# A gated state-space and mixture-of-experts layer: the tile pipeline, the decays and the norm in another order

## The chip, the cores and the metric

The kernel runs on one core of a Trainium2 chip. The metric is the device time of one execution in microseconds (us). The engines of the core work side by side, each through its own queue in order: PE (TensorE, matrix products and transposes), DVE (VectorE), ACT (ScalarE), POOL (GpSimd) and SP (SyncE, which here only issues DMAs). They wait for each other by semaphores. Products land in PSUM, in banks of 128 x 512 float32.

## The reference, cut to what matters

There are four batches of 512 rows and 512 columns. A selective state-space layer runs over a context and is gated with the normed rows; then a mixture of experts runs over the result.

```python
# state-space layer: 512 channels, 16 states each, 512 time steps
u = silu(causal_conv4(in_proj_w @ ctx))
dt_lo, Bm, Cm = split(x_proj_w @ u)
delta = softplus(dt_proj_w @ dt_lo + dt_proj_b)
state = state * exp(delta_t * A) + (delta_t * u_t) * B_t      # for each t
y_t   = sum over the states of state * C_t
y     = (y + D * u) * silu(layernorm(x))
x     = x + tanh(g_xattn) * y
# mixture of experts: one shared, 3 of 7 routed, weighted by their renormed probabilities
h     = layernorm(x)
f(h, w1, wg, w2) = (silu(h @ w1) * (h @ wg)) @ w2
x     = x + tanh(g_ffn) * (f(h, shared) + sum over 3 experts of weight * f(h, expert))
```

All of it is float32.

## The kernel before

**Recurrence** (`loop`, L433). Channels lie on partitions in four chunks `c` of 128, time along the free axis. The 16 states are taken two at a time (`NG`), so one batch has 8 x 4 = 32 *steps*. Step n has these pieces. POOL forms the products `h` = B * (delta u) (`product`, L499). ACT forms two decays exp(delta * A) into PSUM (`decay`, L508; two buffers, `ps_a`). DVE scans twice along time (L533). Then comes `finish` (L456), which runs at the head of the next step: DVE multiplies `h` by C (L465) and adds the two states to `y` (L476). In batch 0, PE adds the states up instead. At the end of the batch each chunk is gated (`gate`, L454). For batches 1 to 3 each decay is issued right before its scan (L532). `finish` also carries pieces of the preparation of the batch after next (`ahead`, L332: projections, convolution, softplus), and issues the next load of B and C rows (`load_bc`).

**Norm** (`post`, L583). For the batch just gated, four row blocks `t` are transposed by PE (L592), added to x by DVE with their statistics (L594 to L596), scaled (`row_scale`, a power on POOL), normed (L604), transposed back (L609) and copied by ACT (L610).

**Experts** (`experts`, L853). `route` (L620) computes the router: product `pl`, transposes `pg`, about forty small DVE operations with an exponential on ACT and the product `pc` in between, ending in `table` (which expert each tile of 128 rows belongs to). POOL then scatters the normed rows into tiles in HBM (L738, 12 DMAs). Meanwhile PE computes the shared expert: four pairs of products `p1s` and `p2s` (`half`), silu by ACT (`sgs`), the multiply by DVE (`hidden`, L880), and the second product `pos` (`second`). Then come 13 tiles, each with three 1 MB weights loaded for its expert. A tile i is cut into three slots of the loop at L954: first `p1`; then the silu, the transpose of the gated rows of tile i-1, and `p2`; then the copy of that transpose (`turned_h`), the multiply h * p2 (L1000), the transpose and copy of the next tile's input (`pt_x`, `turned_x`), and the output product `po` of tile i-1. Two slots later ACT scales it (`out_scaled`, L816), and POOL adds it into HBM by an accumulating scatter (`add_rows`, L821). More tiles than 13 run in a branch (`rest`, L832).

**Order.** The order on each queue is written out by the program: while batch b is in `post` and `experts`, the steps of batch b+1 are put between the slots. The loop at L1063 does this with two running sums. Each slot yields its planned time on PE (tP) and on DVE (tV); steps are issued while tV is behind tP, or once where a slot says so. The tile slots are planned at `SLOT` = 3.5 (L851) and 4.1 us. `moe` (L1029) runs all of `post` for a batch, after its recurrence has ended, and then `experts`.

Of the kernel before, what the change touches and what calls it, by code (L numbers as in the profile page):

```python
# [32 lines left out]
def gated_ssm_moe(  # L33
# [170 lines left out]
    class Layer:  # L204
# [6 lines left out]
        def __init__(self, b, u, delta, y):  # L211
            self.b, self.u, self.delta, self.y = b, u, delta, y
            self.pin, self.pdt, self.z, self.ln = {}, {}, {}, {}
            self.n_rest = self.n_soft = self.n_du = self.n_mul = 0
            self.bcs, self.hs = {}, {}
# [217 lines left out]
    def loop(b, sums):  # L433
# [5 lines left out]
        u, delta, y = ly.u, ly.delta, ly.y  # L439
# [6 lines left out]
        elif nxt is not None:  # L446
            todo = ahead(nxt)
        szs = None
# [7 lines left out]
        def finish(n, h):  # L456
# [9 lines left out]
            if sums is None:  # L466
                if b - 1 in shared_done:
                    cost += next(todo, 0.0)
# [39 lines left out]
        def decay(n, j):  # L508
            g0, c = steps[n]
            da = ps_a.tile([P, L], F32, tag="da", name=f"da_{b}_{g0}_{c}_{j}")  # L510
            nc.scalar.activation(da, delta[:, c, :], AF.Exp, scale=a_neg[:, c, g0 + j : g0 + j + 1])  # L511
            return da
# [3 lines left out]
        for n, (g0, c) in enumerate(steps):  # L516
# [6 lines left out]
            das = []  # L523
            if b == 0:
                das = [decay(n, j) for j in range(NG)]
# [5 lines left out]
            for j in range(NG):  # L531
                da = das[j] if das else decay(n, j)  # L532
                nc.vector.tensor_tensor_scan(h[:, j, :], da, h[:, j, :], 0.0, ALU.mult, ALU.add)  # L533

            if n < last:
                product(ly, n + 1)
            elif nxt is not None and nxt.n_mul > 0:
                product(nxt, 0)
            if b == 0 and g0 == 0:
# [28 lines left out]
        if b == 0:  # L568
            cost += ready(nxt, 0)
            product(nxt, 0)  # L570
        loop_done.add(b)
# [11 lines left out]
    def post(q):  # L583

        b, t0, nt = CHUNKS[q]
# [3 lines left out]
        for t in range(nt):  # L589
            pt = spare(f"pt_{q}_{t}")  # L590
            for c in range(NC):
                nc.tensor.transpose(pt[:, ts(c, P)], y[:, c, ts(t0 + t, P)], ident)  # L592
            x_t = xx[:, t0 + t, :]
            nc.vector.scalar_tensor_tensor(x_t, pt, tg[:, 0:1], x_t, ALU.mult, ALU.add)  # L594
            nc.vector.bn_stats(st[:, t, :], x_t)
            nc.vector.bn_aggr(mv[:, t, :], st[:, t, :])  # L596
            yield 1.7, 1.7
        rstd = row_scale(mv, f"f_{q}")
        xnT = layers[b].u[:, :, 0 : nt * P]
        xns = one.tile([P, NC, D + NW], F32, tag="xn", name=f"xn_{q}")  # L600
        yield 1.5, 1.5, True
        for t in range(nt):
            xn = xns[:, t, 0:D]
            nc.vector.tensor_scalar(  # L604
                xn, xx[:, t0 + t, :], mv[:, t, 0:1], rstd[:, t : t + 1], ALU.subtract, ALU.mult
            )
            pn = spare(f"pn_{q}_{t}").rearrange("p (c q) -> p c q", c=NC)
            for c in range(NC):
                nc.tensor.transpose(pn[:, c, :], xn[:, ts(c, P)], ident)  # L609
            nc.scalar.copy(xnT[:, :, ts(t, P)], pn)  # L610
            yield 1.0, 1.0
# [3 lines left out]
        )  # L615
        normed[q] = xnT, xns
# [3 lines left out]
    def route(q):  # L620
# [28 lines left out]
        nc.scalar.activation(pb, pb, AF.Exp)  # L649
        s2 = tile_("s2", [nt])  # L650
# [118 lines left out]
    def turn(src, what):  # L769
        pt = ps_t.tile([P, NC, P], F32, tag="pt", name=f"pt_{what}")  # L770
# [61 lines left out]
    def rest(q, i, table, n, into):  # L832

        with tc.If(n > i):
# [4 lines left out]
            xT = turned(turn(rows_in(q, i), f"x_{what}"), f"x_{what}")  # L839
# [5 lines left out]
            hT = turned(turn(h, f"h_{what}"), f"h_{what}")  # L845
# [5 lines left out]
    SLOT = 3.5  # L851

    def experts(q):  # L853
# [10 lines left out]
        W = {-1: ws}  # L864
# [4 lines left out]
        def sgs(hc, p1):  # L869
            sg = two.tile([P, L], F32, tag="sg", name=f"sgs_{q}_{hc}")  # L870
            nc.scalar.activation(sg[:, 0:M], p1[:, 0:M], AF.Silu)
            return sg

        def half(k, hc):
            pool, tag = (((ps_h, "p1"), (ps_o, "po")), ((ps_h, "p2"), (ps_t, "pt")))[k][hc % 2]
            return mm(
                pool, tag, f"p{k + 1}s_{q}_{hc}", lambda c: ws.t[k][:, c, ts(hc, P)], lambda c: xnT[:, c, :], M
            )

        def hidden(hc):  # L880
            p2, sg = p2s.pop(hc), sg_s.pop(hc)
            nc.vector.tensor_tensor(hTs[:, hc, :], sg[:, 0:M], p2[:, 0:M], ALU.mult)  # L882


        p2s, sg_s = {}, {}
# [3 lines left out]
        for hc in range(NC):  # L889
            if hc == 0:  # L890
                next(way)
            elif hc > 1:
                next(way, None)
# [228 lines left out]
```

## Time and profile before

| quantity | value |
|---|---|
| three runs | 1179.94, 1183.39 and 1183.77 us; median 1183.39 |
| profiled execution, its own time | 1183.39 us |
| its span, first to last instruction | 1181.3 us |
| PE busy | 962.1 us (81%) |
| DVE busy | 815.8 us (69%) |
| ACT busy | 536.4 us (45%) |
| POOL busy | 471.1 us (40%) |
| mean granted PE clock | 0.929 |
| DMA | 276.29 MB, mean 234 GB/s |

The profile's second part cuts the span into 40 equal slices of 29.5 us; each digit is the busy share in tenths, and PEclk is the PE clock that was granted. Rows of groups give a line, an engine, an operation, what it writes and reads, how often, and the mean time of one. A row of waits names who waited, for whom, and for how long in total, how often and at most. In a row of the timeline the square bracket says how long the engine had been idle before it, and what ended that. PE's ends are modelled, since its products are pipelined.

### The profile page before, as it was taken

Reading aid. Unit: us, or ns where it says so; the run is one execution under the profiler, and the core shown is the slowest. Engines: PE = TensorE matmul, PEld = TensorE weight load, DVE = VectorE, ACT = ScalarE, POOL = GpSimd, SP = SyncE. Lnnn points to the kernel's source line nnn. Section 1 sums busy time; section 2 is a strip of 40 time slices with the busy share of each in tenths; the row PEclk is TensorE's granted clock in tenths of the full one; section 3 lists DMA queues with packets and bytes.
Section 4 is the critical chain, followed back from the end, with each engine's and each line's share of the span. In section 5 each row is a group of like instructions: output and inputs, shape, how many; then the busy total and the mean of one; then the engine's idle time right before and its main releaser. Section 6 shows DMA issues by size and latency. Waiting matters only on the chain. (4 is left out here: it accounts for less than half of the span.)

```text
span 1181.3 us, 8876 instructions
## 1 busy us (share of the span) xinstructions
PE 962.1 (81%) x2504; PEld 431.3 (37%) x2504; DVE 815.8 (69%) x1093; ACT 536.4 (45%) x746; POOL 471.1 (40%) x311
## 2 busy tenths in 40 slices
PE   7475654889998973989998875888998959999995
PEld 3121222334443432434443333333444434444442
DVE  5888995788977787779977787979898723100000
ACT  5654332337667661436676662336566511112211
POOL 0256641463453534464554442645556314011111
PEclk9689896989999996999998896999999989999998
DMA  4169210487988981399997781587998935889994
GB/s 128 41 225 376 78 67 18 173 259 241 337 305 266 316 272 45 142 306 305 339 301 263 274 274 44 195 291 260 314 363 300 312 88 205 287 288 320 314 322 102
DMA packets 138426, 276.29 MB, mean 234 GB/s; under 512 B 17262, under 2 KB 17262, under 8 KB 138110
## 3 DMA queue, kind: packets, MB, share of 16 engines
q1 hardware_dynamic: 126846, 248.91, 60.7%
q0 software_dynamic: 11328, 26.42, 9.3%
q8 instruction: 26, 0.43, 0.1%
q10 hardware_dynamic: 192, 0.26, 0.1%
q14 instruction: 34, 0.28, 0.1%
HBM read 234.85 MB, written 44.91 MB: 237 GB/s over the span
## 5 line engine op out<-in xcount | busy, mean ns | idle before, releaser
L503 POOL TENSOR_TENSOR h<-bc,home 128x1024 f32<-128x1024 f32 x128 | 301.9, 2364 | 356.9 <-DVE home L476 266.4
L783 PE MATMUL p<-w,turned_x 128*128 128x512 f32 x832 | 376.8, 596 | 13.1 <-DMA w<-in_w_dram 7.0
L533 DVE TENSOR_TENSOR_SCAN h<-da,h 128x512 f32<-128x512 f32 x256 | 298.5, 1207 | 73.4 <-ACT da L511 67.5
L783 PE MATMUL po<-w,turned_h 128*128 128x512 f32 x416 | 199.7, 625 | 30.0 <-ACT turned_h L777 30.0
L511 ACT ACTIVATE da<-home,a_neg 128x512 f32<-128x512 f32 x256 | 171.2, 687 | 114.8 <-DVE h L533 113.0
L783 PEld LDWEIGHTS p<-w,turned_x 128*128 128x128 f32 x832 | 153.3, 191 | 191.1 <-issue 173.5
L821 POOL DMA_INDIRECT acc<-yo,row x52 | 94.4, 1816 | 189.9 <-ACT yo L816 153.3
L1000 DVE TENSOR_TENSOR h<-h,p 128x512 f32<-128x512 f32 x52 | 35.1, 674 | 155.0 <-PE p L783 151.2
L476 DVE TENSOR_TENSOR home<-home,h 128x512 f32<-128x512 f32 x192 | 134.8, 702 | 5.8
L465 DVE TENSOR_TENSOR h<-h,bc 128x1024 f32<-128x1024 f32 x96 | 125.8, 1310 | 1.2
L783 PEld LDWEIGHTS po<-w,turned_h 128*128 128x128 f32 x416 | 79.3, 200 | 117.0 <-issue 82.9
L474 PE MATMUL sum<-hc,ident 128*128 128x512 f32 x128 | 72.0, 693 | 54.1 <-DVE hc L465 54.1
L816 ACT ACTIVATE yo<-po,weight 128x512 f32<-128x512 f32 x52 | 35.7, 686 | 130.4 <-PE po L783 130.4
L738 POOL DMA_INDIRECT xs<-xn,place x48 | 58.6, 1220 | 89.7 <-issue 73.2
L777 ACT COPY turned_x<-pt_x 128x512 f32<-128x512 f32 x52 | 30.5, 586 | 119.8 <-PE pt_x L772 119.5
L924 PE MATMUL pos<-w_s,home 128*128 128x512 f32 x128 | 59.4, 620 | 7.8 <-DVE home L882 6.1
L511 ACT ACT_TABLE_LOAD x49 | 62.9, 1283 | 1.7 <-ACT xd L252 0.7
L474 PEld LDWEIGHTS sum<-hc,ident 128*128 128x128 f32 x128 | 24.1, 208 | 101.0 <-DVE hc L465 81.6
L783 PE MATMUL p1s<-home,w_s 128*128 128x512 f32 x128 | 60.0, 613 | 0.0
L783 PE MATMUL p2s<-home,w_s 128*128 128x512 f32 x128 | 57.9, 594 | 1.2 <-DVE home L882 1.1
L984 ACT ACTIVATE h<-p 128x512 f32<-128x512 f32 x52 | 31.1, 597 | 60.7 <-PE p L783 60.5
L984 ACT ACT_TABLE_LOAD x39 | 50.0, 1283 | 16.0 <-PE p L783 15.4
(136 smaller groups left out, 796.8 us busy)
## 6 DMA issues: line engine op xcount, KB each, us to landing
w<-in_w_dram SPq DMA_DIRECT2D x104, 1024.0 KB, 7.5
w<-in_wg_dram SPq DMA_DIRECT2D x52, 1024.0 KB, 11.7
bc<-rows SPq DMA_DIRECT2D x32, 1024.0 KB, 8.4
xt<-xs SPq DMA_DIRECT2D x52, 256.0 KB, 6.3
xs<-empty SPq DMA_DIRECT2D x6, 1560.0 KB, 16.0
w_s<-in_ws_dram SPq DMA_DIRECT2D x8, 1024.0 KB, 10.5
xx<-in_x_dram SPq DMA_DIRECT2D x4, 1024.0 KB, 9.6
w_s<-in_wsg_dram SPq DMA_DIRECT2D x4, 1024.0 KB, 12.8
```

The costliest lines, as they stand in the source:

```text
L465: nc.vector.tensor_tensor(hc, h, bc[:, 1], ALU.mult)
L474: nc.tensor.matmul(sums[c], ident, hc[:, j, :], start=False, stop=(g0 + j == NS - 1))
L476: nc.vector.tensor_tensor(y[:, c, :], y[:, c, :], h[:, j, :], ALU.add)
L503: nc.gpsimd.tensor_tensor(h, layer.bcs[g0][:, 0], layer.u[:, c, :].unsqueeze(1).to_broadcast([P, NG, L]), ALU.mult)
L511: nc.scalar.activation(da, delta[:, c, :], AF.Exp, scale=a_neg[:, c, g0 + j : g0 + j + 1])
L533: nc.vector.tensor_tensor_scan(h[:, j, :], da, h[:, j, :], 0.0, ALU.mult, ALU.add)
L738: put = nc.gpsimd.indirect_dma_start(xs[q % 2], bass.IndirectOffsetOnAxis(ap=place[:, t, k : k + 1], axis=0), xns[:, t, :], None)
L783: nc.tensor.matmul(p[:, 0:n], lhs(c), rhs(c), start=(c == 0), stop=(c == NC - 1))
L816: nc.scalar.activation(yo, po, AF.Copy, scale=slot_of[q][0][:, i : i + 1])
L821: nc.gpsimd.indirect_dma_start(acc, bass.IndirectOffsetOnAxis(ap=slot_of[q][1][:, i : i + 1], axis=0), yo, None, compute_op=ALU.add,)
L924: nc.tensor.matmul(pos[t], hTs[:, c, ts(t, P)], ws.t[2][:, c, :], start=(c == 0), stop=(c == NC - 1))
L984: nc.scalar.activation(h, p1, AF.Silu)
```

## The change

Five things change in the order of the work. The arithmetic stays.

1. A decay pair belongs to a layer and a step (`decay(layer, n)`), and is issued after the scans of the step before, also across two batches.
2. A tile is still three slots, with the stages placed as follows: `gated(i-1)`, `copy_h(i-2)` and `p1(i)`; then `out(i-3)`, the next input's transpose and `p2(i)`; then its copy, the silu, `turn_h(i-1)`, `output(i-2)` and `add_rows` for tile i-3. Two slots follow the last tile. Weight loads move with their buffers' last readers. The shared expert is regrouped in the same way, and the router's sum gets a slot after its exponential. In the branch `rest`, two transposes use other PSUM banks.
3. `post` works on pairs of row blocks in six pieces, with more planned steps between.
4. `moe` issues pieces of the next batch's `post` after each slot of `experts`, as soon as that batch's recurrence has ended.
5. `SLOT` goes from 3.5 to 3.75; the pieces of `ahead` are issued one or more per step, by how many are left.

```diff
         def finish(n, h):
...
                 if b - 1 in shared_done:
-                    cost += next(todo, 0.0)
+                    left = max(n_todo - done[0], 0)
+                    for _ in range(max(1, -(-left // max(1, len(steps) - NC - n)))):
+                        done[0] += 1
+                        cost += next(todo, 0.0)
...
-        def decay(n, j):
+        def decay(layer, n):
             g0, c = steps[n]
-            da = ps_a.tile([P, L], F32, tag="da", name=f"da_{b}_{g0}_{c}_{j}")
-            nc.scalar.activation(da, delta[:, c, :], AF.Exp, scale=a_neg[:, c, g0 + j : g0 + j + 1])
-            return da
+            layer.das[n] = []
+            for k in range(g0, g0 + NG):
+                da = ps_a.tile([P, L], F32, tag="da", name=f"da_{layer.b}_{k}_{c}")
+                nc.scalar.activation(da, layer.delta[:, c, :], AF.Exp, scale=a_neg[:, c, k : k + 1])
+                layer.das[n].append(da)
...
-            for j in range(NG):
-                da = das[j] if das else decay(n, j)
+            for j, da in enumerate(ly.das.pop(n)):
                 nc.vector.tensor_tensor_scan(h[:, j, :], da, h[:, j, :], 0.0, ALU.mult, ALU.add)
             if n < last:
                 product(ly, n + 1)
+                decay(ly, n + 1)
             elif nxt is not None and nxt.n_mul > 0:
                 product(nxt, 0)
+                decay(nxt, 0)
...
     def post(q):
...
+        each(turn_y, pairs[0])
+        yield 1.6, 0.0
+        for k, pair in enumerate(pairs):
+            each(add_y, pair)
+            if k + 1 < len(pairs):
+                each(turn_y, pairs[k + 1])
+                yield 1.6, 3.2
         rstd = row_scale(mv, f"f_{q}")
...
+        yield 0.0, 3.4, True
+        each(norm, pairs[0])
+        yield 0.0, 1.4
+        for k, pair in enumerate(pairs):
+            if k > 0:
+                each(copy_xn, pairs[k - 1])
+            else:
+                for more in pairs[1:]:
+                    each(norm, more)
+            each(turn_xn, pair)
+            yield 1.8, (1.4 if k == 0 else 0.0)
+        each(copy_xn, pairs[-1])
...
     def route(q):
...
         nc.scalar.activation(pb, pb, AF.Exp)
+        yield
         s2 = tile_("s2", [nt])
...
-    SLOT = 3.5
+    SLOT = 3.75
...
         for hc in range(NC):
...
+            if hc > 0:
+                sgs(hc - 1)
+            next(way, None)
+            half(0, hc)
+            yield part, (2.8 if hc == 1 else 0.0), hc == 1
+            if hc > 0:
+                hidden(hc - 1)
+            next(way, None)
             if hc == 1:
...
+            half(1, hc)
+            yield part, (0.4, 4.8, 0.7, 0.7)[hc], hc < 3
...
+        def gated(i):
+            nc.vector.tensor_tensor(hs[i], hs[i], p2.pop(i), ALU.mult)
+        def turn_h(i):
+            pth[i] = turn(hs.pop(i), f"h_{q}_{i}")
+        def copy_h(i):
+            hT[i] = turned(pth.pop(i), f"h_{q}_{i}")
+        def output(i):
+            po[i] = mm(ps_o, "po", f"po_{q}_{i}", lambda c: hT[i][:, c, :], lambda c: W[i].t[2][:, c, :])
+        def out(i):
+            yos[i] = out_scaled(q, i, po.pop(i))
+        for i in range(last_tile + 1):
+            if i > 0:
+                gated(i - 1)
+            if i > 1:
+                copy_h(i - 2)
+            p1[i] = mm(ps_h, "p1", f"p1_{what}", lambda c: xT[i][:, c, :], lambda c: W[i].t[0][:, c, :])
...
+            if i > 0 and i + 1 <= last_tile:
                 W[i + 1].load(1)
+            if i > 2:
+                W[i - 1].load(2)
...
+            yield SLOT, 0.7
+            if i > 2:
+                out(i - 3)
+            if i < last_tile:
+                ptx[i + 1] = turn(xt.pop(i + 1), f"x_{q}_{i + 1}")
+            p2[i] = mm(ps_h, "p2", f"p2_{what}", lambda c: xT[i][:, c, :], lambda c: W[i].t[1][:, c, :])
...
+            yield SLOT + 0.6, 0.0
+            if i < last_tile:
+                xT[i + 1] = turned(ptx.pop(i + 1), f"x_{q}_{i + 1}")
+            hs[i] = two.tile([P, D], F32, tag="sg", name=f"h_{what}")
+            nc.scalar.activation(hs[i], p1.pop(i), AF.Silu)
+            flush()
+            if i > 0:
+                turn_h(i - 1)
+            if i + 2 <= last_tile:
+                W[i + 2] = tile_weights(q, i + 2, table)
+                W[i + 2].load(0)
+            if i > 1:
+                output(i - 2)
+            if i > 2:
+                add_rows(q, i - 3, yos.pop(i - 3))
             if i == last_tile:
+                W[i].load(2)
...
+            yield SLOT + 0.6, 0.0
         i = last_tile
+        gated(i)
+        out(i - 2)
+        copy_h(i - 1)
+        output(i - 1)
+        turn_h(i)
+        yield SLOT + 0.6, 0.7
+        add_rows(q, i - 2, yos.pop(i - 2))
+        copy_h(i)
+        out(i - 1)
+        output(i)
+        yield SLOT, 0.0
+        add_rows(q, i - 1, yos.pop(i - 1))
+        out(i)
+        add_rows(q, i, yos.pop(i))
...
     def moe():
+        posts = [post(q) for q in range(len(CHUNKS))]
...
-            yield from post(q)
+            yield from posts[q]
             banks = SOME
-            yield from experts(q)
+            for slot in experts(q):
+                yield slot
+                if q + 1 < len(CHUNKS) and CHUNKS[q + 1][0] in loop_done:
+                    others, banks = banks, SOME[:2]
+                    piece = next(posts[q + 1], None)
+                    banks = others
+                    if piece is not None:
+                        yield piece
```

## The prediction

> **What bounds the kernel now.** I read the busy shares in slices first, then the busy time by stage, then the waits inside one stage, then single rows. The slices show where engines idle:
>
> ```profile
> PE   7475654889998973989998875888998959999995
> DVE  5888995788977787779977787979898723100000
> PEclk9689896989999996999998896999999989999998
> ```
>
> Until slice 6 only the recurrence of batch 0 runs. From slice 33 on only the tiles of batch 3 run, and PE is full. Between them lie batches 0 to 2, where neither engine is: each dip of PE (slices 7, 16 and 25) is the norm ahead of a batch. I cut the span there, with columns of span, then busy of PE, weight load, DVE, ACT and POOL, PE clock, DMA share and GB/s:
>
> ```profile
> 261.00:454.00 193.00, 166.68 (x447) 75.47 (x447) 161.69 (x196) 122.21 (x168) 86.25 (x40) 0.95 0.84 276
> 454.00:466.00 12.00, 3.53 (x16) 3.16 (x17) 11.12 (x19) 0.00 (x0) 3.45 (x3) 0.64 0.16 56
> 466.00:523.00 57.00, 50.07 (x131) 22.27 (x129) 47.24 (x81) 21.35 (x29) 31.00 (x30) 0.98 0.54 189
> 523.00:713.50 190.50, 167.54 (x448) 76.03 (x448) 159.19 (x191) 121.05 (x166) 85.39 (x39) 0.94 0.88 290
> 783.00:951.00 168.00, 152.27 (x412) 70.27 (x411) 136.83 (x159) 96.54 (x129) 81.11 (x37) 0.97 0.92 307
> 951.00:962.60 11.60, 1.99 (x17) 1.73 (x16) 6.88 (x15) 0.69 (x1) 2.70 (x3) 0.88 0.31 53
> 1016.80:1163.00 146.20, 143.25 (x404) 67.06 (x404) 9.99 (x18) 28.54 (x49) 17.16 (x11) 1.00 0.91 291
> ```
>
> Three stages repeat in each batch: a front (454 to 466 for batch 1: add, norm), the shared expert with the routing (466 to 523), and 13 tiles (523 to 713). The last row is the same 13 tiles with nothing beside them: 11.2 us a tile, PE busy 98%. In batches 0 to 2 the tiles take 193, 190 and 168 us, while DVE idles 31 us in each. In the two engines' waits in 523 to 713 (total, times, longest) the same name stands on both sides:
>
> ```profile
> DVE h L533 <- ACT da L511: 22.7, 9, 6.0
> PE po L783 <- ACT turned_h L777: 11.2, 4, 5.2
> ```
>
> ACT is only 64% busy there. It works in order: a decay queues behind tile work, and a copy for PE behind decays. One instance:
>
> ```profile
> 660.76 1.42 DVE L476 TENSOR_TENSOR home<-home,h 128x512 f32<-128x512 f32 x2
> 663.91 1.15 ACT L291 ACTIVATE ln<-z 128x512 f32<-128x512 f32 x2
> 666.36 1.30 ACT L511 ACTIVATE da<-home,a_neg 128x512 f32<-128x512 f32 x2
> 667.15 2.34 DVE L533 TENSOR_TENSOR_SCAN h<-da,h 128x512 f32<-128x512 f32 x2 [4.97 <-ACT da L511]
> 667.60 0.57 ACT L777 COPY turned_h<-pt_h 128x512 f32<-128x512 f32 x1
> 668.23 6.09 PE L783 MATMUL po<-w,turned_h 128*128 128x512 f32 x8 [5.24 <-ACT turned_h L777]
> ```
>
> DVE is through at 662.2 and stands until 667.15; PE stands 5.24 us for a copy of 0.57 us behind the same decays, then runs its eight matmuls in 6.09 us where unbroken tiles take 3.44. So the tiles of batches 0 to 2 are bound by this coupling, not by an engine.
>
> **The change part by part.** "Step" is one pass of the recurrence on DVE: multiply 1.22, two adds 1.42, two scans 2.34, together 4.98 us.
>
> *Decays a step ahead.* No instruction is added. The decay of step n+1 now follows scan n in ACT's queue. A decay buffer is still freed only by a scan (two buffers), so the lead is what DVE does in between, 2.64 us; it covers two decays (1.30) and one table load (1.28). What is queued behind the waiting decay is ACT's tile work (silu, copies, `out`), and PE waits for that. I expect it bearable, because each of these now has a slot (some 3.9 us of PE) before its consumer. Bounds per tile phase: nothing gained, or all 31 us of DVE's idle.
>
> *A slot between producer and consumer.* Work per tile is the same: 24 matmuls at 0.43 us (eight in 3.44) and two transposes of 0.44, 11.2 us. `gated` of tile i goes from its third slot to the first of tile i+1, `output` one tile later. The third weight of a tile is asked for after its buffer's last reader; before, SP stood 124 us in 434 to 713 on just that (its wait for `po`), with the other loads behind it. Exception: the last tile's third weight is issued one slot (about 5 us) before use, and 1 MB took 7.5 us to land. In batches 0 and 1 that hides under DVE's rest; in 2 and 3 I charge 2 and 1 us (at most 5).
>
> *What a tile phase is then worth.* Each is counted to the gate that ends the next recurrence (batch 2: to its last matmul). Batch 0: DVE 161.7 less one step that moved into the front, 157. Batch 1: PE 145.6, plus 13.7 for the next batch's projections (32 matmuls at 0.43), less two outputs that now lie behind the gate (7) = 152; DVE 159.2 less two steps = 149. Batch 2: 145.6 of tiles and 5.5 of transposes moved in (1.94 at 953.6 and 3.67 at 962.7 in batch 3's norm now) = 151. On each I put half of the idle before, since two engines near the same load don't mesh perfectly: 15.5, 15.5, and 8 for PE in batch 2 (168 less 152.3), and there the 2 us above. That gives **172, 168, 161** for 193, 190, 168.
>
> *The rule against it.* The Trainium skill, "ScalarE: Activation LUTs", section "What ACT_TABLE_LOAD costs", charges 2.66 us for every switch of tables, drain included. The changed order still switches about twice a tile. In 523 to 713 there are 29 loads; at 1.38 us more each, ACT's 121 us would be 161, nothing could be hoped for from reordering, and I would leave 190 (some 20 us more on the sum). But the row says 1283 ns, and at 591.67 a load of 1.28 us is followed by a decay at 592.97: no drain. I take the row.
>
> *DMA.* The tiles of batches 0 to 2 move 53, 55 and 52 MB (GB/s times span). At 172, 168 and 161 us that is 310 to 328 GB/s. By the shares of 0.84, 0.88 and 0.92 the engines would be full at 162, 168 and 155 us: hardly any room. "Perfetto Trace Analysis", section "Identifying the Most-Contended Engine", holds that occupancy of the 16 engines misleads and bytes count. The trace leans that way: a stretch from 835 to 885 moved 345 GB/s at 0.98, one from 1060 to 1110 only 322 at 0.99 with PE hardly waiting. At 345 the floors are 154, 160 and 150, below my sum. I take those; by occupancy I would add 10.
>
> *The fronts* grow, since `post` now issues a second step (batch 2: a third) before the norm. Batch 1, from the gate: scans 2.34, four adds with statistics 6.4 (0.72, 0.69, 0.18 each), a step with one product 5.7, small ones: 15. But `rstd` on POOL now stands behind the last two accumulating scatters, each waiting for the one before to land (8.4 us median): about 19, for 11.2 before. Batch 2: `rstd` stands ahead of these, but there are three steps: 21 for 11.1. Batch 0: the longer steps of the start give 24 for 19.3. The steps themselves are not lost; they were taken off above.
>
> *Shared expert.* The router's exponential, waited for 3 to 5.4 us before, gets a step to hide it. But a step now also stands before the table: in batch 1 the table is ready 28.6 us after the first `pn` instead of 22.5. The 12 scatters on POOL (4.7 us per three, with two products of 2.35 between) end at 52 instead of 48.5, then 5.3 to the load and 2.7 to the transpose as at 514 to 522: first tile after 61.5 us, not 57.9. Batch 2 likewise 61.5 (58.5); batch 0 65 (64.7).
>
> *Batch 3's norm* goes between batch 2's last tiles, where DVE is out of steps. From 951.0 to the router at 967.0 were 16 us; 3 remain (the branch cost PE 2.5). Its transposes are counted above.
>
> **Sum** (us): 177 unchanged, 24 + 65 + 172, 19 + 61.5 + 168, 21 + 61.5 + 161, 3, and 215 for batch 3 (214.3 before) = 1148, against 1181.3. The profiled run took 1183.4, also the median of the three, so 2.1 lie outside the span: **1150 us**.
>
> **Rivals.** (a) *Both waits vanish*: tile phases at their floors 157, 152, 151, 41 us less: **1109**. For it: 11.2 us a tile in batch 3; against: DVE and PE both near full. (b) *DMA becomes the bound*: a whole tile phase can't be held over a share of 0.95: 171, 176, 163: **1159**. For it: 0.92 in batch 2 already; against: the 345 GB/s above. (c) *The change does not do what it says*: a lead of 2.64 us is eaten as soon as a silu (1.28 + 0.60) or a logarithm comes between, DVE's waits for decays stay (15.0, 22.7, 15.5 in the three phases). Floors plus the full idle, 188, 183, 167: **1187**. Against: most instances have one such piece, not two. (d) *Slower: the coupling turns round.* Decay n+1 holds ACT until scan n is done, one scan later than before. If DVE is the later engine, PE waits for copy and silu behind it; the tile phases stay at 193, 190, 173.5 (transposes included), and the longer fronts are paid: **1206**. It decides as soon as the three phases together shrink by less than 17 us. For it: DVE is the fuller engine in batch 0; against: the slot of slack.
>
> **How the numbers follow.** Forecast 0.44 (own range 1130 to 1168), (a) 0.14, (b) 0.17, (c) 0.09, (d) 0.16. A measurement tells about 0.3% from no change. Faster: the first three, and 0.02 of (c): 0.77; within 0.3%: 0.04 of (c); slower: 0.19. The range of 1105 to 1200 leaves out the upper part of (d), about 0.10, and 0.04 below.
>
> **What would show it.** Tile phases near 170 with DVE's waits for decays under 10 us each; PE waits for the hidden copy gone; fronts of about 20 us with `rstd` late in batch 1; the router of batch 3 within 5 us of the last tile. The prediction is wrong if PE's waits in the tiles go up, with ACT waiting for scans (that is (d)), or DMA stands at 0.95 with waits for weights (b).

## The result, and the profile after

The changed kernel takes **1187.84 us** (median of 11 runs, 1186.84 to 1192.22), the kernel before 1183.77 us (11 runs beside it, 1179.94 to 1186.34). The ratio is 1.0044, with a 95% interval of 1.0029 to 1.0059: slower by 0.4%, where 1150 us, 3% faster, was forecast. The time is inside the range of 1105 to 1200; the direction is wrong. The profiled execution has a span of 1184.9 us (before 1181.3).

The busy shares in slices of the kernel after:

```profile
PE   7366651787799994887989986986998989999994
DVE  5888999748689998676889978778999703100000
```

The dips of PE (slices 7, 16 and 25) are still there, the one of slice 33 is gone, and between them PE is hardly fuller than before. The span cut into the stages of the forecast (span, then busy of PE, weight load, DVE, ACT and POOL, PE clock, DMA share, GB/s), with the last tiles of batch 3 at the end:

```profile
267.10:452.30 185.20, 165.54 (x429) 74.11 (x430) 162.96 (x197) 120.28 (x163) 85.10 (x39) 0.94 0.81 268
452.30:473.30 21.00, 8.62 (x32) 4.46 (x31) 16.27 (x23) 5.72 (x8) 8.88 (x6) 0.74 0.84 254
473.30:533.50 60.20, 52.87 (x132) 23.75 (x132) 43.37 (x81) 22.11 (x29) 29.86 (x30) 0.93 0.46 172
533.50:715.40 181.90, 162.90 (x422) 72.04 (x423) 154.22 (x186) 113.97 (x156) 76.67 (x36) 0.95 0.82 270
797.40:971.40 174.00, 154.47 (x444) 73.53 (x444) 138.77 (x168) 87.20 (x121) 76.72 (x36) 0.97 0.86 285
1022.50:1168.00 145.50, 142.93 (x407) 67.95 (x408) 9.99 (x18) 29.27 (x50) 17.29 (x12) 1.00 0.91 291
```

Beside the forecast (us; a tile phase runs from the first tile's first product to the gate that ends the next recurrence, in batch 2 to the last matmul of its tiles):

| stage | before | forecast | after |
|---|---|---|---|
| batch 0: front, shared, tiles | 19.3, 64.7, 193.3 | 24, 65, 172 | 27.9, 62.2, 185.2 |
| batch 1: front, shared, tiles | 11.2, 57.9, 190.0 | 19, 61.5, 168 | 21.0, 60.2, 181.9 |
| batch 2: front and shared, tiles | 69.4, 168 | 82.5, 161 | 82, 174 |
| batch 3: last tile to router, rest | 16, 214.3 | 3, 215 | 3.3, 210.2 |

The fronts cost what was foreseen, but for 4 us more in batch 0, and batch 3's norm is hidden as foreseen. The tile phases did shrink in batches 0 and 1, by 8 us each, 13 and 14 us less than forecast, and batch 2 grew by 6: 541 us in all three, where 501 were forecast and 551 had been before.

The waits say where they went. From the page's costliest groups (busy and mean ns, then the engine's idle time before them and its releaser), the scans, the decays and the matmuls of the first two products:

```profile
L826 PE MATMUL p<-w,turned_x 128*128 128x512 f32 x832 | 394.9, 620 | 50.0 <-ACT h L1053 46.4
L519 ACT ACTIVATE da<-home,a_neg 128x512 f32<-128x512 f32 x256 | 174.7, 690 | 316.2 <-DVE h L539 314.9
L539 DVE TENSOR_TENSOR_SCAN h<-da,h 128x512 f32<-128x512 f32 x256 | 298.3, 1206 | 4.2 <-POOL h L508 2.9
```

and the same operations in the kernel before, with the output product:

```profile
L783 PE MATMUL p<-w,turned_x 128*128 128x512 f32 x832 | 376.8, 596 | 13.1 <-DMA w<-in_w_dram 7.0
L533 DVE TENSOR_TENSOR_SCAN h<-da,h 128x512 f32<-128x512 f32 x256 | 298.5, 1207 | 73.4 <-ACT da L511 67.5
L783 PE MATMUL po<-w,turned_h 128*128 128x512 f32 x416 | 199.7, 625 | 30.0 <-ACT turned_h L777 30.0
L511 ACT ACTIVATE da<-home,a_neg 128x512 f32<-128x512 f32 x256 | 171.2, 687 | 114.8 <-DVE h L533 113.0
```

The scans' idle time fell from 73.4 to 4.2 us, which is what the change was to do. In exchange ACT now stands 315 us before decays (113.0 before), and PE stands 46.4 us for the silu of a tile, a wait that does not show in the kernel before. The waits inside 533.5 to 715.4 (total, times, longest):

```profile
ACT da L519 <- DVE h L539: 51.8, 28, 5.6
PE p L826 <- ACT h L1053: 15.1, 7, 3.5
DVE h L998 <- ACT h L1053: 13.2, 4, 3.8
```

One instance from the timeline (start, duration, engine, operation, idle before it):

```profile
590.83 2.33 DVE L539 TENSOR_TENSOR_SCAN h<-da,h 128x512 f32<-128x512 f32 x2
592.08 0.69 ACT L519 ACTIVATE da<-home,a_neg 128x512 f32<-128x512 f32 x1 [4.84 <-DVE h L539]
593.20 0.69 ACT L519 ACTIVATE da<-home,a_neg 128x512 f32<-128x512 f32 x1 [0.42 <-DVE h L539]
593.82 0.58 ACT L820 COPY turned_x<-pt_x 128x512 f32<-128x512 f32 x1
594.41 1.28 ACT L1053 ACT_TABLE_LOAD   x1
595.70 0.60 ACT L1053 ACTIVATE h<-p 128x512 f32<-128x512 f32 x1
596.33 0.69 DVE L998 TENSOR_TENSOR h<-h,p 128x512 f32<-128x512 f32 x1 [3.17 <-ACT h L1053]
596.35 4.97 PE L826 MATMUL p<-w,turned_x 128*128 128x512 f32 x7 [3.46 <-ACT h L1053]
```

ACT stands idle for 4.84 us in front of a decay whose buffer the scan at 590.83 still holds, with the next x's copy and the silu queued behind. Both are ready to run: their products on PE ended before ACT went idle at 587.24. When the scans let it go, ACT works through two decays, the copy, a table load and the silu, and until 596.3 both PE (whose next first product needs the one bank that the silu reads) and DVE (whose multiply `gated`, the gate of a tile, needs the silu) stand still.

### The profile page after: what moved, and what is told of

Read it like the earlier page. It is cut to its first block, busy times and chain, and to the rows that moved or that the text cites. A ratio compares the mean times of both kernels' runs of the same rounds, so it can differ in the third digit from the quotient of the medians.

```text
span 1184.9 us, 8934 instructions
## 1 busy us (share of the span) xinstructions
PE 963.1 (81%) x2504; PEld 429.2 (36%) x2504; DVE 813.1 (69%) x1093; ACT 531.6 (45%) x742; POOL 469.3 (40%) x311
## 5 line engine op out<-in xcount | busy, mean ns | idle before, releaser
L508 POOL TENSOR_TENSOR h<-bc,home 128x1024 f32<-128x1024 f32 x128 | 305.5, 2387 | 392.5 <-DVE home L481 277.5
L826 PE MATMUL p<-w,turned_x 128*128 128x512 f32 x832 | 394.9, 620 | 50.0 <-ACT h L1053 46.4
L519 ACT ACTIVATE da<-home,a_neg 128x512 f32<-128x512 f32 x256 | 174.7, 690 | 316.2 <-DVE h L539 314.9
L539 DVE TENSOR_TENSOR_SCAN h<-da,h 128x512 f32<-128x512 f32 x256 | 298.3, 1206 | 4.2 <-POOL h L508 2.9
L826 PEld LDWEIGHTS p<-w,turned_x 128*128 128x128 f32 x832 | 158.6, 198 | 242.0 <-issue 176.1
L826 PE MATMUL po<-w,turned_h 128*128 128x512 f32 x416 | 191.6, 604 | 13.7 <-ACT turned_h L820 7.4
L466 DVE TENSOR_TENSOR h<-h,bc 128x1024 f32<-128x1024 f32 x96 | 121.2, 1263 | 0.9
L826 PE MATMUL p1s<-home,w_s 128*128 128x512 f32 x128 | 61.5, 625 | 6.4 <-ACT sgs L924 6.4
L781 POOL DMA_INDIRECT xs<-xn,place x48 | 54.2, 1129 | 29.1 <-issue 15.9
L519 ACT ACT_TABLE_LOAD x50 | 64.2, 1283 | 1.3 <-ACT xd L252 0.4
L959 PE MATMUL pos<-w_s,home 128*128 128x512 f32 x128 | 55.9, 594 | 3.2 <-ACT sgs L924 3.2
L820 ACT COPY turned_h<-pt_h 128x512 f32<-128x512 f32 x52 | 30.1, 579 | 53.3 <-PE pt_h L815 53.3
L233 DVE SCALAR_TENSOR_TENSOR home<-pin,pr,home 128x511 f32<-128x511 f32 (+2 forms) x48 | 35.7, 748 | 22.3 <-ACT home L229 21.1
```

The lines of the kernel that those rows point to most:

```text
L233: nc.vector.scalar_tensor_tensor(xc[:, k:], pin[:, 0 : L - k], pr[:, c, last - k : last - k + 1], xc[:, k:], ALU.mult, ALU.add,)
L466: nc.vector.tensor_tensor(hc, h, bc[:, 1], ALU.mult)
L508: nc.gpsimd.tensor_tensor(h, layer.bcs[g0][:, 0], layer.u[:, c, :].unsqueeze(1).to_broadcast([P, NG, L]), ALU.mult)
L519: nc.scalar.activation(da, layer.delta[:, c, :], AF.Exp, scale=a_neg[:, c, k : k + 1])
L781: put = nc.gpsimd.indirect_dma_start(xs[q % 2], bass.IndirectOffsetOnAxis(ap=place[:, t, k : k + 1], axis=0), xns[:, t, :], None)
L820: nc.scalar.copy(t, pt)
```

## Experiments

Each ratio is to the kernel before, timed beside the run on the same chip. The first theory was that the place of the silu behind waiting decays is the loss. Two rivals stood against it: that two engines near the same load idle for each other whatever the order on ACT, and that the longer fronts ate the gain. Four runs took the change apart.

**The silu one slot earlier.**

```diff
             if i > 2:
                 out(i - 3)
+            hs[i] = two.tile([P, D], F32, tag="sg", name=f"h_{what}")
+            nc.scalar.activation(hs[i], p1.pop(i), AF.Silu)
             if i < last_tile:
                 ptx[i + 1] = turn(xt.pop(i + 1), f"x_{q}_{i + 1}")
 ...
                 xT[i + 1] = turned(ptx.pop(i + 1), f"x_{q}_{i + 1}")
-            hs[i] = two.tile([P, D], F32, tag="sg", name=f"h_{what}")
-            nc.scalar.activation(hs[i], p1.pop(i), AF.Silu)
```

> The kernel after, with the silu of tile i moved from its third slot to its second (behind the scaled output of tile i-3, ahead of the transpose of the next x). Theory (one order on ACT: silu i lies behind decays that wait for a scan, and both p1 of the next tile and the gate of this one wait for it): PE's wait of p for the silu (15 to 17 us per tile phase) falls under 6, DVE's wait of the gate under 5, the tile phases come to about 172, 170 and 163 us instead of 185, 182 and 174, the whole to 1150 to 1160 us. Rival 1 (DVE and PE near the same load idle for each other whatever the order on ACT): the waits only change their names, 1180 to 1190. Rival 2 (the loss sits in the longer fronts): no change either, 1180 to 1190.

Measured: 1170.82 us, ratio 0.9893 (0.9865 to 0.992); tile phases 180, 173 and 171 us. Both waits for the silu are gone. Both rivals had expected no change of the time, and 17 us speak against them. But the time fell by 17 us and not by 28 to 38, because the wait moved to the next piece in ACT's queue, the copy of the turned x:

```profile
L826 PE MATMUL p<-w,turned_x 128*128 128x512 f32 x832 | 390.3, 614 | 35.4 <-ACT turned_x L820 33.9
L519 ACT ACTIVATE da<-home,a_neg 128x512 f32<-128x512 f32 x256 | 174.0, 689 | 271.1 <-DVE h L539 269.6
```

**The decays late again.**

```diff
             if n < last:
                 product(ly, n + 1)
-                decay(ly, n + 1)
             elif nxt is not None and nxt.n_mul > 0:
                 product(nxt, 0)
-                decay(nxt, 0)
 ...
             product(nxt, 0)
-            decay(nxt, 0)
```

A step then issues its own decays, as its loop already did for a step without any.

> The kernel after, with the decays issued as in the kernel before, right ahead of the scans of their own step; all else as after. Theory: the waits for the silu (46 us on PE, 29 on DVE) fall to less than half, DVE's waits for the decays come back to 30 us or more, and the two trade about evenly: 1185 +-8. If the decays ahead were worth what the forecast gave them, it is slower than after by 15 us or more: 1200. If the decays ahead are the whole harm and the slots a gain, 1155 to 1165.

Measured: 1168.2 us, ratio 0.9874 (0.9852 to 0.9897); tile phases 174.0, 175.5, 174.5. So the decays ahead cost 20 us here, 3 us above the case "the whole harm", and the even trade that the theory expected is wrong. PE's wait for the silu is 3.3 us and DVE's for decays 16.7, not 30 or more; what is new is that PE waits 22.9 us for the gate behind DVE's steps. The order of work on PE, DVE, GpSimd and SP is the same as in the changed kernel; only ACT's differs. ACT's idle time before decays is 179.7 us instead of 314.9:

```profile
L823 PE MATMUL p<-w,turned_x 128*128 128x512 f32 x832 | 394.8, 620 | 33.0 <-DVE h L995 22.9
L539 DVE TENSOR_TENSOR_SCAN h<-da,h 128x512 f32<-128x512 f32 x256 | 298.2, 1206 | 29.0 <-ACT da L519 16.7
L519 ACT ACTIVATE da<-home,a_neg 128x512 f32<-128x512 f32 x256 | 172.9, 688 | 181.8 <-DVE h L539 179.7
```

**The decays ahead, alone, in the kernel before.** The edit is the diff's own for `decay` and its calls, with nothing else of the change:

```diff
             if n < last:
                 product(ly, n + 1)
+                decay(ly, n + 1)
```

> The kernel before, with nothing but the decays issued one step ahead. Theory: the waits for decays (53 us in three tile phases) vanish, but here the copy of the turned h has no slot in hand and waits behind decays that wait for scans: PE's waits grow by more, 1190 to 1205. Forecast's reading (the lead is worth half of the idle time by itself): 1145 to 1165. Neither: within 5 us of before.

Measured: 1246.71 us, ratio 1.0536 (1.0517 to 1.0556): 63 us slower, in the direction of the theory and three times its size. Tile phases 219.8, 208.4 and 179.8.

```profile
L534 DVE TENSOR_TENSOR_SCAN h<-da,h 128x512 f32<-128x512 f32 x256 | 298.1, 1206 | 14.0 <-POOL h L503 7.3
L514 ACT ACTIVATE da<-home,a_neg 128x512 f32<-128x512 f32 x256 | 174.1, 689 | 302.8 <-DVE h L534 301.9
L787 PE MATMUL po<-w,turned_h 128*128 128x512 f32 x416 | 222.0, 684 | 77.0 <-ACT turned_h L781 76.9
```

Scans wait 14 us instead of 73.4, so the decays are early as meant; PE's wait for the copy of the turned h went from 30.0 to 76.9. The part of the change that the forecast counted as its gain is a loss by itself in that kernel.

**The norm in one piece.** In the kernel after, `post` and the place where it is issued are those of the kernel before:

```diff
-            yield from posts[q]
+            yield from post(q)
             banks = SOME
-            for slot in experts(q):
-                yield slot
 ...
+            yield from experts(q)
```

> The kernel after, with the norm ahead of a batch as before: one piece after the other tile by tile, and not set between the last tiles of the batch ahead. Theory: the fronts lose 3 to 6 us each at most, since what they grew by is mostly the extra steps of the recurrence that stand there, batch 3 pays its 13 us again: 1183 to 1195. Rival 2 (the fronts are where the gain went): they fall back to 19, 11 and 11 us, 27 us less, against 13 more for batch 3: 1170 to 1176.

Measured: 1198.7 us, ratio 1.0128 (1.0108 to 1.0148), slower than after by 11 and above the theory's band. Fronts of 17.9, 22.8 and 35.3 us: only batch 0's fell, so the rival of the fronts is out. Batch 3 pays 16.1 us from the last tile to the router again, 13 more; fronts and shared experts together are 12 us longer, and the tile phases 14 us shorter (527 us), most of it in batch 2, which no longer carries the next norm.

**More buffers for the decays, first try.** A decay ahead waits for a scan only because there are two buffers. Decays of odd states get two more, in SBUF:

```diff
-                da = ps_a.tile([P, L], F32, tag="da", name=f"da_{layer.b}_{k}_{c}")
+                where, tag = ((ps_a, "da"), (two, "das"))[k % 2]
+                da = where.tile([P, L], F32, tag=tag, name=f"da_{layer.b}_{k}_{c}")
```

> The kernel after in its own order of instructions; the one change is that decays have four buffers in place of two (those of even states in the two PSUM banks as before, those of odd states in two buffers of SBUF), so that a decay one step ahead need not wait for the scan in between. Theory (the harm is that a decay ahead holds ACT's queue until the scan before it has freed its buffer): ACT's waits for scans (50 us per tile phase) fall under 10, PE's and DVE's waits for the silu (46 and 29 us) under 10, tile phases 168 to 174 us, the whole 1150 to 1162. Rival (the order on ACT is the harm even without the wait, since decays stand ahead of the silu): the silu waits stay over 30 us, 1178 to 1190. Further rival (a scan that reads SBUF, or ACT writing there, is slower): scans of over 1206 ns mean; each 0.1 us on 256 scans is 26 us of DVE, some 20 on the time.

Measured: 1283.38 us, ratio 1.0841 (1.0793 to 1.0888). The further rival came true: the scans' mean went from 1206 to 1799 ns, 152 us more of DVE. (The last section reads the rows.) So this run tells nothing of the waits. The same holds for the two others with these buffers (scans of 1799 and 1848 ns): together with the earlier silu,

> The two edits together, four decay buffers and the silu in its earlier slot. Theory: with the wait for scans gone little is left for the silu's place: within 6 us of four buffers alone, 1147 to 1160. Rival (the place on ACT is what counts): 17 us below four buffers alone, as much as the earlier silu gave by itself.

which took 1282.09 us (ratio 1.0818, 1.0772 to 1.0864), and the same four buffers in the kernel before with decays ahead,

> The kernel before with the decays one step ahead, which alone cost 63 us, now with four decay buffers (two in PSUM, two in SBUF). Theory: without the wait for the scan the 63 us go, and DVE's waits for decays (53 us) stay away: 1150 to 1180. Rival (decays ahead do harm by their place in the queue): over 1210.

which took 1259.45 us (1.0616, 1.0566 to 1.0666).

**More buffers, without GpSimd's product.** The slow scans were those that ran beside GpSimd's product. Two runs leave that product out, so that their only difference is the buffers:

```diff
-            nc.gpsimd.tensor_tensor(
-                h, layer.bcs[g0][:, 0], layer.u[:, c, :].unsqueeze(1).to_broadcast([P, NG, L]), ALU.mult
-            )
+            nc.gpsimd.memset(h, 1.0)
```

> The kernel after with GpSimd's product of a step (input times B, 2.35 us) replaced by a plain fill of its target with ones: it leaves out that multiplication, everything else and the two decay buffers stay. It is the base for the next run. Expected of each theory: the product is not on the path (GpSimd is 40% busy and waits for DVE), so 1175 to 1190, scans 1.17 to 1.21 us each, ACT's waits for scans and PE's for the silu as in after.

> The same without the product, and with four decay buffers (two of them in SBUF). In the run of four buffers with the product, a scan that read its decay from SBUF took 2.38 us where GpSimd's product of 2.35 us ran beside it and 1.17 where none did, so that run told nothing of the waits. Theory (decays ahead do harm because they hold ACT until a scan frees their buffer): scans at 1.2 us again, ACT's waits for scans under 60 us in place of 315, PE's and DVE's waits for the silu under 15 each, 20 to 30 us below the run without the product: 1150 to 1165. Rival (the place in ACT's queue is the harm, waiting or not): within 8 us of it. Rival (reading SBUF is slow whatever GpSimd does): scans stay at 1.8 us in the mean, 1270 or more.

Measured: 1177.28 us without the product (ratio 0.996, 0.9947 to 0.9974), and 1132.74 us with four buffers as well (0.9592, 0.956 to 0.9624): **45 us** from the buffers alone, with the same work in the same order on every engine, and more than the 20 to 30 that were expected. PE's own busy time is 15 us shorter (960.2 and 945.2 us, at a mean granted clock of 0.930 and 0.944); no run here tells what moved the clock. The two pages, first with two buffers:

```profile
L824 PE MATMUL p<-w,turned_x 128*128 128x512 f32 x832 | 392.8, 617 | 51.7 <-ACT h L1051 47.7
L517 ACT ACTIVATE da<-home,a_neg 128x512 f32<-128x512 f32 x256 | 174.7, 690 | 311.1 <-DVE h L537 309.6
L537 DVE TENSOR_TENSOR_SCAN h<-da,h 128x512 f32<-128x512 f32 x256 | 298.3, 1207 | 1.6 <-POOL h L508 1.1
```

and with four:

```profile
L825 PE MATMUL p<-w,turned_x 128*128 128x512 f32 x832 | 387.8, 611 | 20.2 <-DVE h L997 11.8
L538 DVE TENSOR_TENSOR_SCAN h<-da,h 128x512 f32<-128x512 f32 x256 | 298.4, 1207 | 3.7 <-POOL h L508 3.7
L518 ACT ACTIVATE da<-home,a_neg 128x512 f32<-128x512 f32 x256 | 174.7, 702 | 134.2 <-DVE h L538 132.8
```

PE's wait for the silu went from 47.7 to 2.9 us, DVE's from 29.6 to none. ACT still stands 133 us before decays, where under 60 was expected: it now runs a step further ahead and waits there without making PE or DVE wait. The tile phases are 164, 168 and 170 us, 501 together, 35 less than with two buffers (537). The forecast's sum was 501 too, but with 172, 168 and 161, and for a kernel that has the product: that the sums agree is in part luck, since an error of 8 us in batch 0 and one of 9 in batch 2 cancel. In this pair, then, it is the wait for the scan that costs, not the place in the queue. Late decays were not run without the product, so whether decays ahead with buffers enough are also better than late ones is not shown.

**The slots alone.** Decays late and the norm in one piece; the tiles' new order stays, and with it the shared expert's, the slot's price of 3.75 and the pieces of `ahead` (part 5 of the change).

> The change without two of its three parts: decays late and the norm in one piece, both as in the kernel before; only the tiles with a slot between producer and consumer (with their DMA order and shared expert) are new. Theory (the parts add): late decays gave 1168 from 1188, the whole norm costs 11, so 1179, 4 us under before. Rival (the slots alone hold the gain of the forecast, the norm in pieces is what it was paid with): 1160 or less. Rival (they are worth nothing without the other parts): 1184 to 1190.

Measured: 1198.82 us, ratio 1.0148 (1.012 to 1.0176), outside all three expectations: the slots alone are a loss of 16 us, and the parts do not add. With the norm whole, late decays gain nothing (1198.7 against 1198.8); with late decays, the norm in pieces gains 31. The loss is not in the tiles: their three phases are 530 us, 21 less than in the kernel before. The fronts, 74 us together for 42, and the shared experts, 188 for 181, take back more. The timeline of this run shows a part of why slots need the new norm. At the end of batch 1's tiles the last outputs lie behind the recurrence's last gate (708.64 us), and the transposes that feed the next norm's adds stand behind them and a branch on PE, until 727.16:

```profile
714.50 3.70 PE L790 MATMUL po<-w,turned_h 128*128 128x512 f32 x8 [1.25 <-ACT turned_h L784]
720.70 3.67 PE L790 MATMUL po<-w,turned_h 128*128 128x512 f32 x8 [2.06 <-SPq L841]
...
728.28 0.75 DVE L600 SCALAR_TENSOR_TENSOR xx<-pt,tg,xx 128x512 f32<-128x512 f32 x1 [5.42 <-PE pt L598]
```

The fronts of batches 1 and 2 are 24.9 and 31.7 us here, and 20.0 and 20.8 with the norm in pieces, which sets the transposes ahead of those outputs (batch 0's front goes the other way, 17.2 here and 28.4 with pieces). The largest single part of the 31 us is batch 3's norm, 13. Why late decays gain nothing in this company is only half seen: PE waits 40.7 us for the gate and the scans 40.8 us for decays, where with decays ahead PE waits 25.6 us for the silu and 14.1 for the gate, and DVE 22.3 for the silu.

**Late decays and the early silu together, and then the gate early too.**

> The kernel after with decays issued late (as in the kernel before) and the silu in its earlier slot. Late decays alone gave 1168. Theory: what was left there on PE was the wait for the gate behind DVE's steps (23 us) and 3 us for the silu; the earlier silu helps only the second: 1160 to 1168. Rival (both edits take away different waits and add): 1150.

Measured: 1169.47 us, ratio 0.9875 (0.9827 to 0.9923): the two do not add, as the theory had it, 1.5 us above its band; PE now waits 30.2 us for the gate. So the gate was moved from the first slot of the next tile to the third slot of its own:

```diff
-            if i > 0:
-                gated(i - 1)
             if i > 1:
                 copy_h(i - 2)
 ...
             if i > 0:
                 turn_h(i - 1)
+            gated(i)
```

> An attempt at a better kernel: decays late, the silu in the second slot, and the gate of tile i behind it in the third slot in place of the next tile's first, so that the bank of p2 comes free a slot earlier. Late decays with the early silu gave 1169, where PE still waits for the gate 5 to 10 us per tile phase. If that wait is on the path: 1150 to 1162. If DVE only waits for p2 in its place, since the gate now stands ahead of its steps: 1168 to 1185.

Measured: **1156.09 us**, ratio 0.9773 (0.9743 to 0.9803), faster than both kernels, by 2.3% than the one before, and inside the first case. Its tile phases (the last row ends 3 us before the last matmul of batch 2's tiles, at 939.57; to there it is 169.5 us):

```profile
267.10:439.10 172.00, 162.60 (x439) 73.59 (x439) 159.50 (x194) 134.02 (x176) 80.16 (x39) 0.98 0.89 295
518.50:687.80 169.30, 156.42 (x415) 70.60 (x415) 150.38 (x185) 127.81 (x167) 74.68 (x36) 0.96 0.88 291
770.10:936.60 166.50, 150.73 (x438) 72.03 (x439) 137.75 (x170) 93.10 (x127) 72.32 (x36) 0.98 0.89 295
```

ACT is busier here than in the changed kernel (134.02 us against 120.28 in batch 0) and the phase is 13 us shorter: ACT's load was not the limit.

**The decays ahead in the best version.** The edit is the one of "decays late", reversed.

> The best version so far (1156: decays late, silu in the second slot, gate in the third) with the decays one step ahead again, as the change has them. Theory (a piece on ACT that stands behind waiting decays is late by up to a step, and only more room before its consumer helps): the silu and the gate now have room, the copy of the turned x has none, so PE waits for that copy some 25 to 35 us (34 in the run with the early silu alone): 1163 to 1175. If the room is what counted and the decays are then harmless: 1150 to 1158. If decays ahead are harm of their own, whatever the room: 1175 or more.

Measured: 1191.54 us, ratio 1.0091 (1.006 to 1.0122): 35 us lost, beyond the theory's 7 to 19 and in the case of a harm whatever the room. More room for silu and gate does not help while others stand behind the decays: PE waits 40.0 us for the copy of the turned x and 21.3 for the scaled output that frees its bank.

```profile
L519 ACT ACTIVATE da<-home,a_neg 128x512 f32<-128x512 f32 x256 | 174.7, 690 | 296.1 <-DVE h L539 294.7
L826 PE MATMUL p<-w,turned_x 128*128 128x512 f32 x832 | 389.1, 613 | 40.7 <-ACT turned_x L820 40.0
L826 PE MATMUL po<-w,turned_h 128*128 128x512 f32 x416 | 197.3, 619 | 29.2 <-ACT yo L859 21.3
```

**The price of a slot.** The best version with `SLOT = 3.5` in place of 3.75.

> The best version so far (1156) with the planner's price of a slot at 3.5 us, as in the kernel before, in place of 3.75; it moves where steps of the recurrence fall between slots and nothing else. No theory of the decays speaks of it; if the place of steps is not critical: 1151 to 1161.

Measured: 1166.58 us, ratio 0.9866 (0.9837 to 0.9894), 10 us more than with 3.75 and outside the 5 that were allowed. Where the planner sets a step between slots is worth about 10 us, so a part of this size may be due to it in the runs that move slots or norm, the loss of the slots alone included: no run took part 5 out of the change by itself. It is no part of the pairs with decays late and ahead, or with two and four buffers: the order of work on PE and DVE is the same in both kernels of each.

## Why the prediction was wrong

**The step that failed** is "Decays a step ahead": "What is queued behind the waiting decay is ACT's tile work (silu, copies, `out`), and PE waits for that. I expect it bearable, because each of these now has a slot (some 3.9 us of PE) before its consumer." It named the queue and the waiters rightly and priced the wait wrongly. A decay ahead is held for up to a step of DVE (4.84 us in the instance above, 5.6 at most in that tile phase), and two decays then go first. In the instance the copy, the table load and the silu take 2.46 us and could have ended near 589.7, by an estimate from the rows shown; they ended at 596.30, 9.1 us after ACT had gone idle. The slot of 3.9 us that was to cover this was there, and PE was through with it at 592.89.

Priced by runs, the decays ahead cost 63 us in the kernel before, 20 in the changed one and 35 in the best version. Beside the early silu (1 us, with overlapping intervals) and beside the whole norm nothing can be told. They gained in none of the five pairs. The pair without GpSimd's product says why: there the same order was 45 us faster as soon as the decays had four buffers in place of two. Rival (d), which the forecast gave 0.16, has the mechanism: "Decay n+1 holds ACT until scan n is done". By its own point of decision it is the one that came true, since the phases shrank by 10 us together and not by 17; its size of 1206 was too high, since it had them not shrink at all. Rival (c), 1187, is nearest in time and wrong in its reason: its waits for decays did vanish. That the measured time lies inside the range of 1105 to 1200 is owed to these rivals, which the range takes in, and not to the forecast.

**The tile phases.** "On each I put half of the idle before" was therefore the term that was missed: 185.2, 181.9 and 174 for 172, 168 and 161, 40 us together, where the whole span came out 37 us too long. The decays ahead are 17 of these 40: with decays late, the three phases are 524 us. With decays late, half of the idle is still 23 us too much to ask; a part of them shows as PE's wait for the gate behind DVE's steps, 22.9 us in that run. The best version, which moves the silu and the gate, has 1.9 us of this wait and phases of 511 us. What holds the last 10 us is open; batch 2 is the phase that stays too high (169.5 for 161).

**What was foreseen and came.** DVE's waits for decays are 1.1, 0 and 0.2 us in the three phases (under 10 each was forecast). In 533.5 to 715.4 PE no longer waits for the copy of the turned h, 11.2 us before. No wait for a weight shows on PE, and DMA stands at 0.81, 0.82 and 0.86, so rival (b) did not come; in the best version, at 0.88 to 0.89, PE waits 4.9 us for weights in all. The router of batch 3 starts 3.3 us after the last tile (3 forecast). Batches 1 and 2 together have fronts and shared experts of 163.2 us against 163. In batch 1 GpSimd waits 7.7 us for an accumulating scatter ahead of `rstd`, as said, and DVE only 1.3 us for `rstd` itself.

**What was foreseen and did not come.** SP's wait for `po` was to go, 124 us before. It is now 50.4 us for `po` and 50.5 for the other products in 533.5 to 715.4: the weights still wait 101 us for their buffers, in two places, and no wait of PE for a weight comes of it. Batch 0's front is 27.9 us for 24, its shared expert 62.2 for 65; batch 3's rest is 210.2 for 215.

**The table loads.** The forecast took the row of 1283 ns against the 2.66 us with a drain of the Trainium skill ("ScalarE: Activation LUTs", section "What ACT_TABLE_LOAD costs"), whose sum would have been some 20 us higher and so nearer to the result. The row holds: at 594.41 a load of 1.28 us is followed by the silu at 595.70. The rule would have come near for a reason that no row shows.

The change added up from the kernel before, each on top of the last: the slots with part 5 +16 us; the norm in pieces −31; the decays ahead +20, which leaves the 4 us by which the change is slower. In another order the shares differ (after the slots, the decays ahead 0 and then the norm in pieces −11), so they belong to this order and are not properties of the parts. The three tile phases go 551, 530, 524 and 541 us on this way.

## What to carry to other kernels

Before you issue work one step ahead on an engine that works in order, ask whether it can start there. When its output buffer is freed only by the step in between, it waits at the head of the queue, and everything behind it becomes late by that wait. Read who stands behind, and give it a further buffer before giving it an earlier place; if there is no buffer, leave it behind the work that is ready. And price the delay of a piece by all that stands in front of it in its queue, the wait included (9.1 us here), before comparing it with the slot that is to cover it (3.9 us).

## What the runs showed of the hardware

A scan that reads its decay from SBUF is as fast as one that reads PSUM, 1.17 us, when GpSimd runs no product beside it, and takes about twice as long when it does. Pairs in the run with four decay buffers, the first scan of each from PSUM and the second from SBUF, with GpSimd's product beside them:

```profile
638.37 3.58 DVE L540 TENSOR_TENSOR_SCAN h<-da,h 128x512 f32<-128x512 f32 x2
638.53 2.35 POOL L508 TENSOR_TENSOR h<-bc,home 128x1024 f32<-128x1024 f32 x1 [4.33 <-DVE home L481]
646.69 3.59 DVE L540 TENSOR_TENSOR_SCAN h<-da,h 128x512 f32<-128x512 f32 x2
646.85 2.35 POOL L508 TENSOR_TENSOR h<-bc,home 128x1024 f32<-128x1024 f32 x1 [5.97 <-DVE home L481]
```

and one pair in the run without the product, where GpSimd only fills:

```profile
384.70 2.33 DVE L538 TENSOR_TENSOR_SCAN h<-da,h 128x512 f32<-128x512 f32 x2
384.84 0.95 POOL L508 MEMSET h<- 128x1024 f32 x1 [3.56 <-DVE home L481]
```

The product runs from 646.85 to 649.20; if the second scan starts only then and takes 1.17 us, it ends at 650.37, and the pair ends at 650.28. The Trainium skill, "SBUF — State Buffer", section "SBUF: two separate sides", says just this: DVE with two SBUF inputs and a GpSimd instruction that reads SBUF contend for one pair of ports, which the first takes for its whole instruction while the other stands; a fill, which reads nothing, does not enter. Both rows agree. A decay in PSUM is thus what lets the scans run beside GpSimd's products without standing: with half of them in SBUF the scans took 450.0 us in place of 298.3. That closes the simple way to more decay buffers in this kernel. Two other ways, one more PSUM bank taken from the tiles and decays of half the size, were not tried.
